# One set's value product turned round, POOL's two steps exchanged, and the quantized product fed earlier

## The chip, the cores and the metric

The kernel runs on one core of one Trainium2 chip. Time is the device time of one execution in microseconds (us); of several runs the median is given. A core has the matrix engine (PE, whose weight loads are shown as PEld), VectorE (DVE), ScalarE (ACT), GpSimd (POOL), and SyncE (SP), which here only issues DMA transfers. PE writes to PSUM[...].

## The reference

A small model of six residual blocks works on x (2 sequences of 64 rows, 1024 columns), with a second input ctx (2 x 1024 x 1024). Each block adds to x a function of its layer norm:

```python
x = x + quantized_matmul(layernorm(x), ctx)          # fake_quant on both operands, per tensor
x = x + mamba(layernorm(x))                          # in_proj, conv, chunk scan, gated norm, out_proj
x = x + lora_experts(layernorm(x))
x = x + point_cloud(ctx, layernorm(x))               # two graph layers
x = x + masked_linear(layernorm(x))
x = x + swiglu_ffn(layernorm(x))
```

Two of them matter here. The quantized product rounds both operands to 256 levels and multiplies: `q = clip(round(x / s + z), 0, 255)`, then `(q1 - z1) * s1 @ (q2 - z2) * s2`.

The point cloud sorts 1024 points of each sequence along four space-filling curves. For each point it takes the 10 neighbours on each curve, and forms features relative to the point itself. In each of two layers a self-attention over the 10 neighbours runs, 64 features a head; its output goes through two linear maps, an instance norm, a leaky ReLU and a maximum over the 10:

```python
scores = einsum('bihd,bjhd->bhij', qh, qh) / sqrt(headdim)
attn = softmax(scores); out = einsum('bhij,bjhd->bihd', attn, qh)
fused = out @ W_lin.T + b_lin;  h1 = einsum('oc,bnkc->bonk', W_conv1, fused)
feats1 = lrelu(instance_norm(h1)).max(axis=-1)
```

Half of the features are the point's own and the same for all its neighbours, so that only four heads need attention; the kernel treats the rest as a constant per point ("centre").

## The kernel before, in words

**Quantized product** (`quant_attention`, L176 to L260). ctx comes in four halves of 2 MB, each as two transfers, into two buffers of the pool `op` (tag "ow"), which later hold output weights; `fetch` (L184) asks for the third and the fourth half when a buffer is free again. ctx is worked on in eight pieces of 128 x 2048. ACT scales a piece (`scaled`, L207), VectorE rounds and clamps it in two instructions to bf16 (`rounded`, L211 and L212), and PE multiplies it twice (L250): with ones, for the column sums (`pc`), and with the quantized, transposed x (`po`). At the end ACT and VectorE add both to x (L254, L255, L258). The small parameters of later blocks are asked for in `parameters` (L262), between the second and the third half of ctx on SP's queue. The weights of `in_proj` follow in `project` (L318) from the pool `wp` (tag "w", three buffers).

**Set-up of the point cloud** (`point_cloud`, L1068). `fused_weights` (L761) multiplies the two linear maps of a layer on the chip and splits the product into three bf16 parts `wz`, whose sum is exact enough. POOL fills the buffers x16 and xz with zeros (L1115).

**The steps.** A phase is one layer of one sequence; there are four, of 22 sets of 48 points each (the last set has 16 points), 88 sets in all. A set's data are 16 blocks of 3 points x 10 neighbours, padded to 32 columns, for two pairs of heads: x of 128 x (2, 16, 32). The set i goes through these functions:

- `edges` (L887, POOL): neighbours minus the centre, into one of four x buffers; `mended` (L895) corrects the first set of a phase.
- `apart` (L908): copies each half of the partitions (one head of each pair) into xz, zeros elsewhere, in one of three buffers. ACT does both halves (L916), but in layer 2 VectorE does the second (L914).
- `scores` (L918, PE), `maxima` (L927, VectorE), `exponentials` (L931: PE subtracts the maxima, L934; ACT takes the exponential, L936).
- `normalize` (L938): VectorE sums and inverts (L941, L942), POOL multiplies e (L943).
- `turn` (L945, VectorE): transposes the attention in 32 x 32 blocks (L947).
- `weighted` (L949): PE forms u = features x wz, per block, with the features as weights and wz as moving operand (L960), three parts one on the other; ACT copies u from PSUM (L962).
- `attend` (L964): PE multiplies attention and u (L975) onto the centres (L972); ACT copies (L977). `back` (L979) transposes it, `collect` (L987) takes norm statistics and maxima on VectorE (L996, L998).

`iteration(i)` (L1146) interleaves them for sets i+2 down to i-3. The order of an engine's instructions comes from this order of calls, with some shifts that the scheduler inside one iteration makes; each engine then runs its list in order. The core of it:

```python
edge(i + 2)                                        # POOL
self.mended(at(i + 1)); self.apart(at(i + 1), 1)
self.turn(at(i - 2)); self.collect(at(i - 3))
self.exponentials(at(i - 1)); self.scores(at(i)); self.normalize(at(i - 1))
self.maxima(at(i)); self.apart(at(i + 1), 0); self.attend(at(i - 2))
self.weighted(at(i)); self.back(at(i - 2)); todo(i)
```

`todo` does what is due beside the steps. The gathers of neighbours for the next phase (L861, POOL's DMA queue, 32 a phase) are turned by PE (L871) and copied by ACT into the window `win` (L868, L873), which `edges` reads. The centres (L829 to L840), the norm of a finished phase (L1021) and the masking of a later weight (L1264) are due there too.

Of the kernel before, what the change touches and what calls it, by code (L numbers as in the profile page):

```python
# [12 lines left out]
BF16 = mybir.dt.bfloat16  # L13
I32 = mybir.dt.int32
AF = mybir.ActivationFunctionType
ALU = mybir.AluOpType
# [4 lines left out]
P = 128  # L21
D = 1024
KC = D // P
NB = 2
S = 64
# [17 lines left out]
NBK = SG // TP  # L43
# [49 lines left out]
class Kernel:  # L93
# [82 lines left out]
    def quant_attention(self, sb, op, gp, rp, ps, pout, ppy):  # L176
# [42 lines left out]
        for b in range(NB):  # L219
            for kp in range(4):  # L220
                j = 2 * b + kp // 2
                if kp % 2 == 0 and j >= 1 and j + 1 < 4:
                    fetch(j + 1)
                v = halves[j][:, 2 * (kp % 2):2 * (kp % 2) + 2, :].rearrange("p k n -> p (k n)")
                scaled(v, 1)
                if b == 0 and kp == 0:
                    scaled(h, 0)
                cq = self.t(gp, [P, 2, D], BF16, tag="xc")
                rounded(cq.rearrange("p k n -> p (k n)"), v)
                if b == 0 and kp == 0:  # L230
                    rounded(hq, h)
                    pt = self.t(ps, [P, KC, P], BF16, tag="misc")
                    for c in range(KC):
                        nc.tensor.transpose(pt[:, c, :], hq[:, c * P:(c + 1) * P], id16)
                    nc.scalar.copy(hT, pt)
                if b == 0 and kp == 1:

                    pr = self.t(ps, [P, 1], tag="misc")
                    for c in range(KC):
                        nc.tensor.matmul(pr, hT[:, c, :], ones16[:, 0:1], start=(c == 0), stop=(c == KC - 1))  # L240
                    dd = self.t(sb, [P, 1], tag="dd")
                    nc.vector.tensor_scalar(dd, d[:, 1:2], float(D), None, ALU.mult)
                    nc.vector.tensor_tensor(row, pr, dd, ALU.add)
                    nc.vector.tensor_tensor(row, row, d[:, 3:4], ALU.mult)
                r = slice(S * b, S * (b + 1))
                for dst in (pc, po):
                    for k2 in range(2):
                        kc = 2 * kp + k2
                        for n in range(2):
                            nc.tensor.matmul(dst[r, n, :], ones16 if dst is pc else hT[:, kc, r], cq[:, k2, 512 * n:512 * (n + 1)],  # L250
                                             start=(kc == 0), stop=(kc == KC - 1))
# [28 lines left out]
    def mamba(self):  # L280
# [3 lines left out]
        with ExitStack() as es:  # L284
# [6 lines left out]
            update = self.quant_attention(sb, op, gp, rp, ps, pout, ppy)  # L291
# [469 lines left out]
    def fused_weights(self, layer):  # L761
# [11 lines left out]
        nc.sync.dma_start(wv, a[f"W_conv{layer}"])  # L773
        wz = [self.t(self.g_w, [P, 2, o], BF16, tag=f"wz{layer}{j}") for j in range(3)]
# [13 lines left out]
        nc.vector.tensor_copy(wctr, pt[:65])  # L788
        return wz, wctr
# [159 lines left out]
    def weighted(self, it):  # L949

        nc, xz, nb, layer = self.nc, it["xz"], it["nb"], it["layer"]
        wz, _ = self.gw[layer]
        u = it["u"] = self.t(self.g_a, [P, NBK, 64 * layer], tag="u", bufs=2)
        kb = 8 // layer
        for k0 in range(0, nb, kb):
            pu = self.t(self.g_ps, [P, kb, 64 * layer], tag="misc")
            for k in range(kb):
                for j in range(3):
                    for hp in range(2):
                        nc.tensor.matmul(pu[64 * hp:64 * hp + 64, k, :], xz[:, hp, k0 + k].rearrange("p a j -> p (a j)"), wz[j][:, hp, :],  # L960
                                         start=(j == 0), stop=(j == 2), skip_group_check=True)
            nc.scalar.copy(u[:, k0:k0 + kb], pu)  # L962

# [104 lines left out]
    def point_cloud(self):  # L1068
        nc, tc, a = self.nc, self.tc, self.a
        with ExitStack() as es:  # L1070
# [69 lines left out]
            def edge(i):  # L1140
                it = at(i)
                if it:
                    it["x"], it["xz"] = x16[i % len(x16)], xz[i % len(xz)]
                    self.edges(it)

            def iteration(i):  # L1146


                edge(i + 2)
# [257 lines left out]
```

## Time and profile before

| | us |
|---|---|
| median of 3 runs (lowest to highest) | 1133.85 (1132.46 to 1140.82) |
| profiled execution, its own time | 1180.42 |
| its span | 1178.6 |
| first matmul of in_proj (L325) | at 49.12 |
| step 0 of layer 1 (L934) | at 551.20 |
| step 0 of layer 2 (L934) | at 800.30 |
| last step of layer 2 (L934) | at 1084.60 |

| stage | us | PE | DVE | ACT | POOL | mean PE clock |
|---|---|---|---|---|---|---|
| quantized product, to 49.12 | 49.12 | 24.11 | 30.59 | 21.97 | 0.20 | 1.00 |
| mamba and experts, to 501.60 | 452.48 | 437.15 | 308.53 | 210.17 | 96.76 | 0.99 |
| set-up of the point cloud | 49.60 | 17.07 | 18.29 | 13.85 | 30.13 | 0.57 |
| layer 1 | 249.10 | 206.67 | 143.49 | 193.17 | 189.08 | 0.92 |
| layer 2 | 284.30 | 266.44 | 208.84 | 205.34 | 180.14 | 0.98 |
| the rest | 94.00 | 85.31 | 28.12 | 11.99 | 1.66 | 0.98 |

A line of a group reads: line, engine, operation, tiles written and read, shapes, how often; then busy us and mean ns of one; then the engine's idle time just before these instructions and what ended it. Line numbers are those of the kernel before. The chain of waits gives start, length, and the work or wait that the end hung on. A releaser is inferred; where several waits end together, the last one is named.

### The profile page before, as it was taken

The page shows a single profiled execution, that of the slowest core. Times are in us where ns is not written, and L with a number is a line of the kernel's source. Part 1 is how long each engine was busy: PE and PEld are TensorE (multiplying, and loading weights), DVE is VectorE, ACT ScalarE, POOL GpSimd, SP SyncE. Part 2 cuts the span into 40 slices and gives each one's busy share as a digit, 9 for nine tenths or more (in the row PEclk, how much of TensorE's full clock was granted, in tenths as well). Part 3 has the DMA queues.
Part 4 walks back from the last instruction along what each step waited for, and adds up shares of the span by engine and source line. Part 5 has one row for each costly group of instructions (what it writes and reads, how often), then busy time and mean ns, then how long its engine had stood idle before and what let it go on. Part 6 is the DMA issues. An engine that isn't in the chain of part 4 may idle for free.

```text
span 1178.6 us, 40925 instructions
## 1 busy us (share of the span) xinstructions
PE 1036.7 (88%) x18413; PEld 796.2 (68%) x18413; DVE 737.9 (63%) x1546; ACT 656.5 (56%) x1057; POOL 498.0 (42%) x403
## 2 busy tenths in 40 slices
PE   3799999999999998944887888888999998999998
PEld 1699968869778683533665666667778776878443
DVE  5698966775766755442554565757757658997511
ACT  4433426556565561025886787865877677776110
POOL 0010110110415245346878877765757657852000
PEclk9999999999999999965998988988999999999999
DMA  6777739677695667475011003110121100000360
GB/s 258 297 286 287 328 145 411 248 299 319 242 402 216 288 240 254 168 221 80 13 23 26 14 12 66 24 27 11 32 44 21 26 11 10 12 4 4 144 285 18
DMA packets 48027, 171.41 MB, mean 145 GB/s; under 512 B 26422, under 2 KB 27362, under 8 KB 40940
## 3 DMA queue, kind: packets, MB, share of 16 engines
q1 hardware_dynamic: 37844, 151.74, 34.8%
q10 hardware_dynamic: 3864, 12.82, 3.0%
q0 software_dynamic: 6144, 4.24, 1.8%
q8 instruction: 144, 2.36, 0.8%
q14 instruction: 31, 0.25, 0.1%
HBM read 163.57 MB, written 2.72 MB: 141 GB/s over the span
## 4 chain that ended last, share of the span: by engine, by line
PE 55%; DVE 22%; ACT 9%; issue 6%; POOL 4%; DMA 4%; SPq 0%; ACTq 0%; another core or an unknown queue 0%; DVEq 0%; POOLq 0%
PE misc L960 13%; PE pin L325 8%; PE po L459 7%; PE op L975 5%; DVE cpre L340 4%; PE sc L925 4%; ACT df L732 3%; PE pt L985 3%; PE sc L1288 2%; DVE df L731 2%; POOL x L893 2%; PE misc L1288 2%; PE sc L934 2%; POOL e L943 2%; PE op L972 1%
## 5 line engine op out<-in xcount | busy, mean ns | idle before, releaser
L325 PEld LDWEIGHTS pin<-hT,w 128*128 128x128 f32 x2320 | 260.9, 192 | 4.5 <-issue 3.8
L325 PE MATMUL pin<-hT,w 128*128 128x128 f32 x2320 | 263.0, 275 | 0.9 <-issue 0.4
L960 PE MATMUL misc<-wz,xz 128*64 128x64 bf16 (+1 forms) x8256 | 213.3, 213 | 17.7 <-issue 14.2
L960 PEld LDWEIGHTS <-xz 128*64 128x64 f16 x8256 | 197.9, 115 | 34.4 <-issue 30.4
L893 POOL TENSOR_TENSOR x<-win,cen 128x960 f16<-128x960 f32 x88 | 170.7, 1946 | 73.0 <-PE sc L925 28.6
L962 ACT COPY u<-misc 128x512 f32<-128x512 f32 x258 | 148.6, 586 | 61.3 <-PE misc L960 34.1
L861 POOL DMA_INDIRECT sl<-src,place x128 | 128.1, 1001 | 40.6 <-issue 18.5
L916 ACT COPY xz<-x 64x1024 f16<-64x1024 f16 (+1 forms) x132 | 134.7, 1020 | 8.1 <-POOL x L893 3.4
L947 DVE STREAM_TRANSPOSE at<-e 128x512 f32<-128x512 f32 x88 | 61.4, 698 | 110.9 <-POOL e L943 110.9
L943 POOL TENSOR_TENSOR e<-e,z 128x512 f32<-128x512 f32 x88 | 95.3, 1083 | 75.2 <-DVE z L942 65.9
L439 POOL TENSOR_TENSOR xc<-y,normw 128x512 f32<-128x512 f32 x8 | 8.3, 1036 | 274.1 <-DVE y L437 231.5
L732 ACT ACTIVATE df<-df,neg 128x1024 f32<-128x1024 f32 x64 | 73.4, 1147 | 90.0 <-DVE df L731 85.5
L459 PE MATMUL po<-ow,xc 128*128 128x512 f32 x256 | 115.3, 604 | 1.7 <-DVE acc L467 1.4
L975 PE MATMUL op<-u,at 128*32 128x64 f32 (+1 forms) x2752 | 92.9, 256 | 22.0 <-issue 13.0
L340 DVE SCALAR_TENSOR_TENSOR cpre<-craw,convw,cpre 128x126 f32<-128x126 f32 (+2 forms) x240 | 78.2, 347 | 28.1 <-ACT cpre L334 20.1
L925 PEld LDWEIGHTS <-xz 128*64 128x64 f16 x2752 | 55.8, 115 | 52.4 <-issue 50.7
L975 PEld LDWEIGHTS op<-u,at 128*32 128x32 f32 x2752 | 64.4, 112 | 39.2 <-issue 21.5
L459 PEld LDWEIGHTS po<-ow,xc 128*128 128x128 f32 x256 | 48.2, 193 | 57.8 <-issue 55.2
L715 POOL DMA_INDIRECT place<-cst,rank x64 | 68.2, 1065 | 40.4 <-issue 17.2
L731 DVE SCALAR_TENSOR_TENSOR df<-hi_r,hl,lo_r 128x1024 f32<-128x1024 f32 x64 | 81.7, 1304 | 4.1 <-DMA lo_r<-rows 2.9
L925 PE MATMUL sc<-x,xz 128*64 128x32 f16 x2752 | 68.0, 186 | 7.8 <-ACT xz L916 5.9
L941 DVE TENSOR_REDUCE z<-e 128x16 f32<-128x512 f32 x88 | 58.8, 668 | 22.3 <-ACT e L936 21.1
(327 smaller groups left out, 1398.2 us busy)
## 6 DMA issues: line engine op xcount, KB each, us to landing
w<-in_in_proj_w SPq DMA_DIRECT2D x36, 2048.0 KB
ow<-in_out_proj_w SPq DMA_DIRECT2D x16, 2048.0 KB
w<-in_L_ffn_w SPq DMA_DIRECT2D x3, 4096.0 KB
ow<-in_ctx SPq DMA_DIRECT2D x8, 1024.0 KB
hi_r<-rows ACTq DMA_DIRECT2D x8, 512.0 KB
lo_r<-rows ACTq DMA_DIRECT2D x8, 512.0 KB
df<-in_L_attn_mask ACTq DMA_DIRECT2D x8, 512.0 KB
w<-in_base_W SPq DMA_DIRECT2D x2, 2048.0 KB
```

Source lines behind the costliest of these rows:

```text
L325: nc.tensor.matmul(pt[:, c, :], w[:, c, kc, :], hT[:, kc, :], start=(kc == 0), stop=(kc == KC - 1))
L340: nc.vector.scalar_tensor_tensor(pv[:, :, s:], rv[:, :, :S - s], convw[:, cc + c, 3 - s:4 - s], pv[:, :, s:], ALU.mult, ALU.add)
L459: nc.tensor.matmul(st["po"][:, n, :], st["xc"][:, 4 * q + c, :], ow[:, c, 512 * n:512 * n + 512], start=(q == 0 and c == 0), stop=(q == 1 ...
L732: nc.scalar.activation(df, df, AF.Sign, bias=neg[:, cc:cc + 1], scale=1.0, accum_out=sums[:, c:c + 1])
L861: nc.gpsimd.indirect_dma_start(out=ph[c][:, m, :], out_offset=None, in_=ph["src"][:, :], in_offset=bass.IndirectOffsetOnAxis(ap=k, axis=0))
L893: nc.gpsimd.tensor_tensor(xv, over, mid, ALU.subtract)
L916: nc.scalar.copy(dst, src)
L925: nc.tensor.matmul(sc[64 * hp:64 * hp + 64, k, :], xz[:, hp, k].rearrange("p a j -> p (a j)"), x[:, hp, k, :], start=False, stop=False, sk ...
L943: nc.gpsimd.tensor_tensor(e, e, z.unsqueeze(2).to_broadcast([P, nb, 32]), ALU.mult)
L960: nc.tensor.matmul(pu[64 * hp:64 * hp + 64, k, :], xz[:, hp, k0 + k].rearrange("p a j -> p (a j)"), wz[j][:, hp, :], start=(j == 0), stop= ...
L962: nc.scalar.copy(u[:, k0:k0 + kb], pu)
L975: nc.tensor.matmul(op[32 * r:32 * r + 32, q, :], it["at"][:, 4 * q + r, :], it["u"][:, 4 * q + r, :], start=False, stop=True, skip_group_c ...
```

## The change

Four things change.

1. The four halves of ctx are all asked for at the start, the third and fourth into two buffers of the weight pool `wp`; so all eight transfers stand ahead of the parameters on SP's queue. ACT scales a piece one ahead. PE's product with x (`po`) is held back one piece, until the transposed x is there. The copy of the transposed x and the three small sums for `row` stand later in ACT's and VectorE's order. `pc` is read and added in two halves.
2. For layer 1 `fused_weights` also lays the weights out by head, 64 rows of values and 64 of zeros, in `heads`: a memset on POOL and six copies on VectorE.
3. For layer 1 `weighted` takes these weights as the stationary operand, 32 columns for each of the four heads, and x itself, 512 columns, as the moving one. Each head's 32 output columns land on 32 partitions of PSUM of their own. `turn_u` then transposes them on VectorE, in 32 x 32 blocks, from PSUM into u; ACT copies nothing. Layer 2 is as before.
4. In both layers `edge(i + 2)` stands after `normalize(at(i - 1))` in `iteration`, no longer first.

```diff
         def fetch(j):
-            c = self.t(op, [P, 4, D], tag="ow")
+            c = self.t(op, [P, 4, D], tag="ow") if j < 2 else self.t(wp, [P, 4, D], tag="w")
...
-        fetch(0)
-        fetch(1)
+        for j in range(4):
+            fetch(j)
         self.parameters(sb, rp)
...
+        scaled(piece(0), 1)
+        scaled(h, 0)
+        for i in range(2 * 4):
+            b, kp = divmod(i, 4)
+            if i + 1 < 8:
+                scaled(piece(i + 1), 1)
+            if i == 1:
+                nc.scalar.copy(hT, pt)
+            cq = self.t(gp, [P, 2, D], BF16, tag="xc")
+            rounded(cq.rearrange("p k n -> p (k n)"), piece(i))
...
+            product(pc, b, kp, cq)
+            waiting.append((po, b, kp, cq))
+            if i >= 1:
+                while waiting:
+                    product(*waiting.pop(0))
...
-        nc.scalar.activation(t, pc.rearrange("p a n -> p (a n)"), AF.Identity, bias=row, scale=d[:, 1:2])
-        nc.vector.scalar_tensor_tensor(self.x, t, s12, self.x, ALU.mult, ALU.add)
+        for q in range(2):
+            c = slice(512 * q, 512 * q + 512)
+            nc.scalar.activation(t[:, c], pc[:, q, :], AF.Identity, bias=row, scale=d[:, 1:2])
+            nc.vector.scalar_tensor_tensor(self.x[:, c], t[:, c], s12, self.x[:, c], ALU.mult, ALU.add)
...
+        if layer == 1:
+            heads = self.t(self.g_w, [P, 3, 2, 2, o], BF16, tag="wzh")
+            nc.gpsimd.memset(heads, 0.0)
...
+        if layer == 1:
+            for j in range(3):
+                for h2 in range(2):
+                    r = slice(64 * h2, 64 * h2 + 64)
+                    nc.vector.tensor_copy(heads[r, j, :, h2, :], wz[j][r])
+            wz = heads
...
+        if layer == 1:
+            u = self.t(self.g_a, [P, 2, NBK, 32], tag="u", bufs=2)
+            it["u"] = u.rearrange("p a b o -> p b a o")
+            for ob in range(2):
+                pu = self.t(self.g_ps, [P, NBK, 32], tag="misc")[:, 0:nb]
+                for j in range(3):
+                    for h in range(4):
+                        nc.tensor.matmul(pu[32 * h:32 * h + 32], wz[:, j, h // 2, h % 2, 32 * ob:32 * ob + 32], it["x"][:, h // 2, 0:nb, :],
+                                         start=(j == 0), stop=(j == 2), skip_group_check=True)
+                it["pu"].append((u[:, ob, 0:nb], pu))
+            return
...
+    def turn_u(self, it):
+        for u, pu in it["pu"]:
+            self.nc.vector.transpose(u.rearrange("p b j -> p (b j)"), pu.rearrange("p b j -> p (b j)"))
...
-                edge(i + 2)
                 if at(i + 1):
                     self.mended(at(i + 1))
                     self.apart(at(i + 1), 1)
...
                 if at(i - 1):
                     self.normalize(at(i - 1))
+                edge(i + 2)
                 if at(i):
                     self.maxima(at(i))
...
                 if at(i):
                     self.weighted(at(i))
+                    self.turn_u(at(i))
```

More of the change, by code (lines that the diff above doesn't have):

```diff
@@ L173, in transposed, with quant_attention @@
         return hT
-    def quant_attention(self, sb, op, gp, rp, ps, pout, ppy):
+    def quant_attention(self, sb, wp, op, gp, rp, ps, pout, ppy):
         nc, a = self.nc, self.a
@@ L218, in quant_attention @@
         pc = self.t(ppy, [P, 2, 512], tag="py")
[L219 to L251, printed above, removed]
@@ new lines, in quant_attention, with product @@
+        waiting = []
+        def product(dst, b, kp, cq):
+            r = slice(S * b, S * (b + 1))
+            for k2 in range(2):
+                kc = 2 * kp + k2
+                for n in range(2):
+                    nc.tensor.matmul(dst[r, n, :], ones16 if dst is pc else hT[:, kc, r], cq[:, k2, 512 * n:512 * (n + 1)],
+                                     start=(kc == 0), stop=(kc == KC - 1))
+        piece = lambda i: halves[i // 2][:, 2 * (i % 2):2 * (i % 2) + 2, :].rearrange("p k n -> p (k n)")
@@ new lines, in quant_attention @@
+        scaled(piece(0), 1)
[8 more added lines that the diff above has]
+            rounded(cq.rearrange("p k n -> p (k n)"), piece(i))
+            if i == 0:
+                rounded(hq, h)
+                pt = self.t(ps, [P, KC, P], BF16, tag="misc")
+                for c in range(KC):
+                    nc.tensor.transpose(pt[:, c, :], hq[:, c * P:(c + 1) * P], id16)
+            product(pc, b, kp, cq)
[3 more added lines that the diff above has]
+                    product(*waiting.pop(0))
+            if i == 1:
+                pr = self.t(ps, [P, 1], tag="misc")
+                for c in range(KC):
+                    nc.tensor.matmul(pr, hT[:, c, :], ones16[:, 0:1], start=(c == 0), stop=(c == KC - 1))
+            if i == 2:
+                dd = self.t(sb, [P, 1], tag="dd")
+                nc.vector.tensor_scalar(dd, d[:, 1:2], float(D), None, ALU.mult)
+                nc.vector.tensor_tensor(row, pr, dd, ALU.add)
+                nc.vector.tensor_tensor(row, row, d[:, 3:4], ALU.mult)
@@ L290, in mamba @@
             es.enter_context(tc.manual_schedule(engines=WITH_SP))
-            update = self.quant_attention(sb, op, gp, rp, ps, pout, ppy)
+            update = self.quant_attention(sb, wp, op, gp, rp, ps, pout, ppy)
             convw, convb, normw = self.convw, self.convb, self.normw
@@ L1142, in edge @@
                 if it:
+                    it["pu"] = []
                     it["x"], it["xz"] = x16[i % len(x16)], xz[i % len(xz)]
```

## The prediction

> **What bounds the kernel now.** I read the table of stages first, cut at the matmul that subtracts the maxima (L934), which runs once in each of the 88 steps of the point cloud: steps 0 to 43 (layer 1) from 551.2 us, steps 44 to 87 (layer 2) from 800.3 to 1084.6 us.
>
> ```profile
> core 0: us, PE busy (x) PEld busy (x) DVE busy (x) ACT busy (x) POOL busy (x), PEclk, DMA share, GB/s
> 551.20:800.30 249.10, 206.67 (x7130) 161.83 (x7128) 143.49 (x295) 193.17 (x310) 189.08 (x151) 0.92 0.12 25
> 800.30:1084.60 284.30, 266.44 (x7260) 220.40 (x7260) 208.84 (x341) 205.34 (x347) 180.14 (x136) 0.98 0.09 18
> ```
>
> A step takes 249.1/43 = 5.79 us in layer 1 and 284.3/43 = 6.61 us in layer 2. In layer 2 PE is busy 94% of the time. In layer 1 no engine is full (PE 83%, ACT 78%, POOL 76%), so a chain between engines sets the step, and PE loses time to itself. The groups of layer 1, with the idle time ahead of them in the last column, say which:
>
> ```profile
> L947 DVE STREAM_TRANSPOSE at<-e 128x512 f32<-128x512 f32 x41 | 29.1, 711 | 63.8 <-POOL e L943 63.7
> L893 POOL TENSOR_TENSOR x<-win,cen 128x960 f16<-128x960 f32 x42 | 82.3, 1968 | 27.8 <-ACT win L873 13.7 <-PE sc L925 9.0 <-remote 2.7
> L975 PE MATMUL op<-u,at 128*32 128x64 f32 x1328 | 39.1, 230 | 18.0 <-issue 11.1 <-DVE at L947 6.4
> ```
>
> VectorE's transpose of the attention waits 63.7 us for POOL's normalized e, because POOL does the edges of a later set ahead of it. PE waits 11 us here, and 11 us in the product of u, for "issue". On the chain of waits "issue" is 13.1% of layer 1 and 4.5% of layer 2: 33 + 13 = 45 us.
>
> The quantized product is bound at first by one landing of data, then by a second one that was asked for late; the chain:
>
> ```profile
> 1.65 7.72 DMA ow<-in_ctx
> ...
> 27.89 6.95 DMA ow<-in_ctx
> 34.87 2.10 ACT ow L207
> 36.99 1.24 DVE ow L211
> 38.33 1.24 DVE xc L212
> ```
>
> **What the Trainium skill says.** "TensorE: Matmul & The Clock Gate", Architectural detail: ScalarE's and VectorE's queues are strict FIFO, only PE pulls weight loads ahead. The timeline agrees: both engines run in the program's order, waiting ones included. My main step rests on it. The same page, Part 3: outputs of 32 columns in different column strips run at the same time, three strips 2.38 times as fast as one. The trace agrees: 32 matmuls of L975 in four strips take 0.58 us on the chain, 18 ns each. "SBUF — State Buffer", Who interferes with whom: a VectorE operation with at most one SBUF input outside the two-port modes does not fight POOL for ports. The transpose out of PSUM is such a one; that it reads PSUM no row of before shows, but L947 is 0.70 us with POOL beside it. The first page, Part 1: PE's clock halves after an idle window of about 3.4 us; the trace shows the granted clock at 0.5 in several windows of layer 1 (mean 0.92).
>
> **Part 1, the quantized product.** All eight loads of ctx (1 MB each) are issued at once, two buffers coming from the weight pool. Piece 0 still lands at 9.4 us; at the 415 GB/s of the busy slices a piece takes 2.5 us, so the last lands at 27 instead of 34.9. VectorE needs 1.23 + 1.23 us a piece: from 15.4 us (piece 0 and h done) seven pieces are 17.2 us, with three small ones 33.0, against 39.6 before: -6.6. The y in halves lets VectorE's first half run under ACT's second: -0.5. So **-7** (bounds -8, as in landing at once, and -5, if loads side by side are slower). On SP's queue the seven parameter loads and the first weights now stand behind the ctx loads; parameters are used from 58 us (L334) and land before 27. Of the three weight loads that lie ready at 49 us, the second and third now wait for VectorE's last reading of buffers 2 and 3 (27.7 and 33 us); 2 MB takes 5 us, so they land at about 34 and 39, ahead of PE's first use at 42. If that cover went, PE would wait a few us.
>
> **Part 2, set-up.** Six copies of 0.2 us (as L788) on VectorE, which is the chain there: **+1** (0 to 1.5). POOL's memset of 768 columns, 0.8 us (L1115: 1.0 for 1024), lies before 13.6 us of POOL idle: nothing.
>
> **Part 3, u of layer 1.** PE: 96 matmuls of 64 columns, 1.64 us, become 24 of 512. A 512-column bf16 matmul follows its neighbour in 0.22 us (L934 to L922), so in four strips 6 x 0.22 = 1.3 us: -0.3, between 1.3 and, strip after strip, 5.3. 144 fewer PE instructions of 336 a step should take about half of the "issue" waits of layer 1, some 12 us, off PE. ACT: two copies of 0.587 go, -1.17. VectorE: two transposes of 0.71 (bounds 0.655, the reduction L929 from PSUM, and 1.0) come, after waiting for PE; behind them is queued the turn of the next attention, on which L975 waits. VectorE's sum is then 0.71 + 0.39 + 0.39 + 0.68 + 0.25 + 0.66 + 1.42 = 4.5 us, below the step. All of this would gain if the step were PE's or ACT's. It is not:
>
> **Part 4, POOL's order.** Edges(i+2) now stand behind the normalization of i-1. That e comes early, as wanted, but it closes a circle. Edges(i+2) cannot start before e(i-1). In the next step ACT's first instruction is the copy of those edges (L916), and in its queue the exponential of i stands behind it; VectorE's z(i) and POOL's e(i) follow, and then edges(i+3). One turn is one step. Before, edges stood first and a turn spanned two steps. Steps from start to start:
>
> ```profile
> 553.22 0.60 ACT L936 ACTIVATE e<-sc 128x512 f32<-128x512 f32 x1
> 553.84 1.05 ACT L916 COPY xz<-x 64x1024 f16<-64x1024 f16 x1
> 553.85 0.69 DVE L941 TENSOR_REDUCE z<-e 128x16 f32<-128x512 f32 x1 [7.37 <-ACT e L936]
> 554.57 0.25 DVE L942 RECIPROCAL z<-z 128x16 f32<-128x16 f32 x1
> 554.79 0.57 ACT L962 COPY u<-misc 128x512 f32<-128x512 f32 x1
> 554.97 1.05 POOL L943 TENSOR_TENSOR e<-e,z 128x512 f32<-128x512 f32 x1 [3.38 <-ACT xz L916]
> ...
> 1004.00 0.70 DVE L947 STREAM_TRANSPOSE at<-e 128x512 f32<-128x512 f32 x1
> 1004.74 0.42 DVE L914 COPY xz<-x 64x1024 f16<-64x1024 f16 x1
> 1005.17 0.67 DVE L996 BATCH_NORM_STATS2 st<-pt 128x6 f32<-128x480 f32 x1
> 1005.76 0.64 DVE L998 TENSOR_REDUCE hm<-pt 128x48 f32<-128x480 f32 x1
> 1006.43 0.69 DVE L941 TENSOR_REDUCE z<-e 128x16 f32<-128x512 f32 x1
> 1007.15 0.25 DVE L942 RECIPROCAL z<-z 128x16 f32<-128x16 f32 x1
> ```
>
> Layer 1: edges 1.97 + 0.03 to the waiter, copy 0.95, exponential 0.63, sum 0.72, reciprocal and hop 0.40, e until the edges start 1.01 (744.48 to 745.49): **5.71 us**. Every 2.7 steps ACT's win copy (L873, 0.39) stands in it: 0.14. VectorE has 1.2 us to spare, but its tasks between sets take up to 2.6 us: I take 0.1 (0 to 0.3). So 5.95 x 43 = 256 us, **+7**. Gathers (1.48 a step of 1.28) fit into POOL's wait of 2.7 us. Layer 2: the copy goes by VectorE, ahead of all else: 2.00 + 0.43 + 0.74 + 0.59 + 0.67 + 0.72 + 0.40 + 1.01 = **6.56 us**. With 0.15 for overruns 6.7 x 40, and three steps without edges at 5.77 (the last ones of before), 285 us: **+1**.
>
> **Sum.** -7 + 1 + 7 + 1 = +2 against the profiled execution's 1180.4 us. But the median of the runs is 1133.85, 46.6 us less. The two circles hold no PE instruction, only ACT, VectorE and POOL at work, so they stay as long in a run that PE gets through faster. What PE loses by "issue" on the chain of these two stages is 45 us, of the size of the gap. If all the gap lies there, the loops of before take 533 - 45 and the change costs 47 us; if it is spread evenly, 2. I take half: 1133.85 + 2 + 22 = **1158 us**.
>
> **Rivals.**
> *The circles bind, but no more than the present step (1136).* The gap of 46.6 us lies elsewhere. For it: layer 1's 5.79 is nearly 5.95 already. Against: steps of 5.4 in a row near 645 us and 5.77 at the end show what the engines do undisturbed.
> *A gain: POOL's early e frees the chain (1098).* If the wait of L947 for e is what ends last, layer 1 falls to POOL's own sum, 1.20 + 1.97 + 1.48 x 1.28 = 5.07: 43 x 0.72 = -31, with -7 + 1 that is -37 on 1180, or 1098 on the median. It speaks for it that the wait is the largest of the stage. It decides only where ACT's copy does not wait for the edges, so that 0.65 us of the circle are hidden; the in-order queue excludes that as I read it.
> *Strips do not overlap (about 1230).* Then u costs 5.3 us, PE's step is 7.7 against 5.95, 43 x 1.75 = +75. Against it: L975's 18 ns.
>
> **Numbers.** Forecast 0.59, no more than the present step 0.28, gain 0.09, strips 0.04. Between runs of this kernel about 1% (1122.5 to 1145.2) cannot be told from no change. Slower 0.62, same 0.27, faster 0.11. The range goes from the rival's 1136 less the bounds of parts 1 and 4 (-1 and -8) to the whole gap in the loops with PE at half clock a little more often (1181 + 3): 1127 to 1184.
>
> **What would show it.** Right: first use of in_proj weights (L325 before) at about 42 us; the interval of the maxima matmul near 5.9 in layer 1 with little spread, near 6.6 or more in layer 2; ACT's copy and, in layer 2, VectorE's copy waiting for POOL's edges for tens of us; POOL's e waiting for z; PE's busy share in both stages lower. Wrong: a layer 1 step below 5.6, which would mean the circle is not closed; a product of u over 3 us on PE; or weights late at 42 us.

## The result: slower by 49 us

| | us |
|---|---|
| kernel before, in the same set of runs | 1137.34 (1132.46 to 1141.15) |
| changed kernel | 1186.31 (1184.75 to 1186.62) |
| ratio | 1.043, 95% interval 1.038 to 1.048 |
| profiled execution of the changed kernel, its own time | 1186.53 (span 1184.8) |

The forecast was 1158 with a range of 1127 to 1184: the sign was right, the size half of what came. Runs sent together share a chip, and each ratio below is taken against the kernel before among them; that kernel takes 1134 to 1139 us (medians) in some of these sets and 1176 to 1179 in others, which turns out to be the heart of the matter. I call them short sets and long sets; this result is of a short one.

### The profile page after: what moved, and what is told of

It is laid out like the page before. It is cut to its first block, busy times and chain, and to the rows that moved or that the text cites. A ratio compares the mean times of both kernels' runs of the same rounds, so it can differ in the third digit from the quotient of the medians.

```text
span 1184.8 us, 34694 instructions
## 1 busy us (share of the span) xinstructions
PE 1013.4 (86%) x15341; PEld 743.2 (63%) x15341; DVE 757.0 (64%) x1641; ACT 612.6 (52%) x972; POOL 503.4 (42%) x404
## 4 chain that ended last, share of the span: by engine, by line
PE 29%; DVE 27%; POOL 19%; ACT 13%; issue 5%; DMA 5%; ACTq 0%; POOLq 0%; SPq 0%; DVEq 0%
POOL x L912 13%; PE pin L335 8%; POOL e L962 6%; PE po L469 5%; ACT xz L935 4%; DVE cpre L350 4%; ACT df L742 3%; PE sc L1325 2%; PE misc L991 2%; DVE z L960 2%; DVE at L966 2%; DMA df<-in_L_attn_mask 2%; DVE df L741 2%; PE misc L1325 2%; ACT e L955 2%
## 5 line engine op out<-in xcount | busy, mean ns | idle before, releaser
L912 POOL TENSOR_TENSOR x<-win,cen 128x960 f16<-128x960 f32 x88 | 180.4, 2050 | 2.9 <-ACT win L892 2.8
L962 POOL TENSOR_TENSOR e<-e,z 128x512 f32<-128x512 f32 x88 | 90.5, 1028 | 151.5 <-DVE z L961 102.0
L880 POOL DMA_INDIRECT sl<-src,place x128 | 130.7, 1021 | 42.4 <-issue 17.4
L991 PE MATMUL misc<-wz,xz 128*64 128x128 bf16 x4128 | 125.9, 221 | 1.9 <-ACT u L993 1.0
L991 PEld LDWEIGHTS <-xz 128*64 128x64 f16 x4128 | 118.6, 111 | 11.0 <-issue 10.8
L1010 PE MATMUL op<-u,at 128*32 128x64 f32 (+1 forms) x2752 | 83.1, 268 | 46.6 <-DVE at L966 46.4
L993 ACT COPY u<-misc 128x512 f32<-128x512 f32 x172 | 100.4, 586 | 19.8 <-PE misc L991 11.5
L350 DVE SCALAR_TENSOR_TENSOR cpre<-craw,convw,cpre 128x126 f32<-128x126 f32 (+2 forms) x240 | 78.1, 347 | 28.1 <-ACT cpre L344 22.4
L1020 PE MATMUL pt<-cst,oT 128*128 128x128 f32 x258 | 49.0, 298 | 43.6 <-ACT oT L1012 43.6
L944 PEld LDWEIGHTS <-xz 128*64 128x64 f16 x2752 | 55.4, 117 | 46.8 <-issue 46.8
L980 PE MATMUL misc<-x,wzh 128*32 128x512 f16 (+1 forms) x1056 | 81.9, 455 | 0.6 <-ACT win L892 0.6
```

Of the source, the lines that this page charges most:

```text
L350: nc.vector.scalar_tensor_tensor(pv[:, :, s:], rv[:, :, :S - s], convw[:, cc + c, 3 - s:4 - s], pv[:, :, s:], ALU.mult, ALU.add)
L880: nc.gpsimd.indirect_dma_start(out=ph[c][:, m, :], out_offset=None, in_=ph["src"][:, :], in_offset=bass.IndirectOffsetOnAxis(ap=k, axis=0))
L912: nc.gpsimd.tensor_tensor(xv, over, mid, ALU.subtract)
L962: nc.gpsimd.tensor_tensor(e, e, z.unsqueeze(2).to_broadcast([P, nb, 32]), ALU.mult)
L1010: nc.tensor.matmul(op[32 * r:32 * r + 32, q, :], it["at"][:, 4 * q + r, :], it["u"][:, 4 * q + r, :], start=False, stop=True, skip_group_c ...
```

## The profile after

The stages, cut at the first in_proj product and at the matmul that subtracts the maxima (L953 now). Columns: start and end, length, busy time and instructions of each engine, PE's granted clock, DMA share, GB/s. By count the cut between the two layers lies at the last step of layer 1 (step 43), and the second ends one step before the last; so it was in the table of before too (800.30 and 1084.60), and all kernels here are cut alike.

```profile
core 0: us, PE busy (x) PEld busy (x) DVE busy (x) ACT busy (x) POOL busy (x), PEclk, DMA share, GB/s
...
543.50:806.70 263.20, 194.29 (x4132) 115.95 (x4129) 185.36 (x381) 145.75 (x225) 186.68 (x149) 0.86 0.11 22
806.70:1091.90 285.20, 259.48 (x7260) 217.51 (x7259) 183.47 (x343) 208.75 (x347) 192.35 (x139) 0.99 0.09 18
```

Layer 1 is 263.2 us, 6.12 a step, and layer 2 285.2. PE is busy 74% and 91% of the two; no engine is full in layer 1. The groups of layer 1 (busy time, mean ns of one | idle time just before and what ended it) say where the waiting went:

```profile
L935 ACT COPY xz<-x 64x1024 f16<-64x1024 f16 x80 | 83.4, 1042 | 102.3 <-POOL x L912 94.7 <-DVE x L922 6.8
L912 POOL TENSOR_TENSOR x<-win,cen 128x960 f16<-128x960 f32 x40 | 78.5, 1963 | 0.0
...
L962 POOL TENSOR_TENSOR e<-e,z 128x512 f32<-128x512 f32 x42 | 44.0, 1048 | 64.0 <-ACT xz L935 36.5 <-DVE z L961 23.3 <-ACT oT L1012 4.2
...
L966 DVE STREAM_TRANSPOSE at<-e 128x512 f32<-128x512 f32 x41 | 27.9, 680 | 1.8 <-POOL e L962 1.7
```

In the kernel before, ACT's copy and POOL's e of layer 1 waited far less:

```profile
L916 ACT COPY xz<-x 64x1024 f16<-64x1024 f16 x80 | 83.3, 1042 | 4.7 <-POOL x L893 3.4
L943 POOL TENSOR_TENSOR e<-e,z 128x512 f32<-128x512 f32 x42 | 45.5, 1082 | 18.0 <-DVE z L942 14.3 <-ACT xz L916 3.4 <-issue 0.2
```

VectorE's wait of 63.7 us for e is gone, as POOL's order was to bring about; in its place ACT's copy waits 94.7 us for POOL's edges and POOL's e 64 us, for ACT and VectorE mostly. One turn of the circle, on the chain of waits of layer 1 (start, length, work):

```profile
633.08 1.05 POOL e L962
634.12 1.93 POOL x L912
636.05 0.02 issue
636.08 1.04 ACT xz L935
637.12 0.03 issue
637.14 0.60 ACT e L955
637.74 0.02 issue
637.77 1.05 ACT xz L935
638.82 0.01 POOLq L962
638.83 0.10 issue
638.92 1.05 POOL e L962
```

A turn is 638.92 - 633.08 = 5.84 us without a PE instruction in it. The chain puts ACT's second copy last before e; VectorE's sum and reciprocal (0.68 + 0.25) end within 0.1 us of it. In layer 2 the same is seen on VectorE; the first line is of the kernel before:

```profile
L975 PE MATMUL op<-u,at 128*32 128x128 f32 x1296 | 48.8, 280 | 3.5 <-DVE at L947 1.8 <-issue 1.4
...
L1010 PE MATMUL op<-u,at 128*32 128x128 f32 x1296 | 45.2, 281 | 22.4 <-DVE at L966 22.4
L962 POOL TENSOR_TENSOR e<-e,z 128x512 f32<-128x512 f32 x42 | 44.0, 1048 | 82.8 <-DVE z L961 74.5 <-ACT oT L1012 6.3 <-ACT xz L935 2.0
...
L933 DVE COPY xz<-x 64x1024 f16<-64x1024 f16 x41 | 17.4, 424 | 90.7 <-POOL x L912 90.7
```

PE, which was the bound of layer 2, now waits 22.4 us for the turned attention, where it waited 1.8.

## The experiments

The theories of the first four runs: **A**, the circle that POOL's late order closes sets the time. **B**, the new u of layer 1 costs it (VectorE's transposes, or PE at half clock). The rivals of later runs stand in their expectations. For the size of the loss a second question came up: what the 46.6 us between the profiled execution and the runs of before are.

### Which part costs

`e1_order_only`: the kernel before with only POOL's order changed.

```diff
-                edge(i + 2)
...
                     self.normalize(at(i - 1))
+                edge(i + 2)
```

> The kernel before with POOL's edges put behind the normalization, nothing else changed. Theory A (the circle edges, ACT's or VectorE's copy, exponential, sum, normalization, edges sets the step): layer 1 steps near 6.1 us, layer 2 steps near 6.6 us in the profile, and the whole 50 to 60 us slower than before, 1187 to 1197 us, since the product's 7 to 8 us are not gained. Theory B (the loss comes from u: VectorE's transposes, or PE at half clock because it has less to do): within 10 us of before, 1127 to 1147 us.

`e3_u_only`: the parts 2 and 3 of the change alone. Against the changed kernel, edges come first again and `quant_attention` is that of before:

```diff
+                edge(i + 2)
                 if at(i + 1):
...
                     self.normalize(at(i - 1))
-                edge(i + 2)
...
-        update = self.quant_attention(sb, wp, op, gp, rp, ps, pout, ppy)
+        update = self.quant_attention(sb, op, gp, rp, ps, pout, ppy)
```

> The kernel before with the new u of layer 1 (and its set-up) alone, POOL's order as before. Theory A: the circle is not there; layer 1 steps fall towards POOL's own 5.1 us in the profile, and the whole is between 25 us faster and the same, 1112 to 1138 us. Theory B: most of the loss is here, 1170 to 1195 us.

`e4_order_undone`: the changed kernel with `edge(i + 2)` first again (the first diff backwards).

> The changed kernel with POOL's edges put first again. Theory A: no loss is left; u_only less 7 us, 1105 to 1131 us. Theory B: still slower than before, 1163 to 1187 us.

`e2_quant_only`: the kernel before with the changed `quant_attention` alone.

```diff
-            c = self.t(op, [P, 4, D], tag="ow")
+            c = self.t(op, [P, 4, D], tag="ow") if j < 2 else self.t(wp, [P, 4, D], tag="w")
```

> The kernel before with the reordered quantized product alone. Both theories: first in_proj matmul at about 43.8 us instead of 49.1, 5 to 8 us faster than before, 1129 to 1132 us. If the early start is given back later in the mamba block, 1137.

| before in this set 1139.22 | us | ratio (95%) | layer 1 | layer 2 |
|---|---|---|---|---|
| e1, order alone | 1228.45 | 1.079 (1.073 to 1.084) | 298.7 | 289.5 |
| e3, u alone | 1145.60 | 1.005 (1.002 to 1.008) | 237.5 | 265.1 |
| e4, all but the order | 1140.92 | 1.002 (1.000 to 1.005) | 233.9 | 265.2 |
| e2, quantized product alone | 1130.96 | 0.992 (0.990 to 0.994) | 233.0 | 264.0 |

The order is the cause: taking it back gives 45 us (1186.31 to 1140.92, both in short sets), adding it alone costs 89. That is far more than theory A's 1187 to 1197, and the trace of e1 says why the changed kernel gets off with less (chain of waits, layer 1):

```profile
699.15 1.92 POOL x L893
701.08 0.02 issue
701.10 1.05 ACT xz L916
702.15 0.02 issue
702.17 1.07 ACT u L962 x2
703.24 0.02 issue
703.26 0.41 ACT pm L868
703.68 0.04 issue
703.72 0.69 PE misc L871 x2
```

In the old form of u ACT's two copies from PSUM stand in its queue behind the copy of the late edges; so the chain runs on from there into PE, and steps of 9 to 12 us come between steps of about 4 to 7. The new u takes those copies off ACT and is worth 298.7 - 263.2 = 36 us of layer 1 under the late order. Under the old order it is worth nothing: layer 1 takes 233.9 us with it (e4) and 233.0 without (e2), and by the medians it costs 6 us (e3 against before) to 10 (e4 against e2), of which the traces place some 3 (1 in the set-up, 1 in each layer). Theory A had counted on a gain there, and so e3 and e4 lie 8 and 10 us above its ranges. Theory B falls: they lie 22 us and more below its own. Why layer 1 does not get shorter there stays open; VectorE is at work for 192 of the 234 us, by 49 us more than without.

The loops (the two layers' steps) of the kernel before, unchanged in e2, are 233.0 and 264.0 us here, not the 249.1 and 284.3 of the profile shown ahead of the prediction:

```profile
540.90:773.90 233.00, 196.50 (x7131) 157.16 (x7129) 143.56 (x295) 192.42 (x310) 190.78 (x151) 0.92 0.14 27
773.90:1037.90 264.00, 257.43 (x7260) 216.67 (x7260) 205.97 (x341) 206.95 (x347) 180.18 (x136) 0.99 0.10 19
```

### What the gap of 46.6 us is

`f1_before_again` is the kernel before, unchanged, with a profile of its own. `g1_after_again` is the changed kernel in another set; neither has an edit.

> The kernel before, unchanged, for a second profile. It decides on the term of +22 in the prediction's sum. Theory A (the first profiled execution was slow in the two loops, and its loops are else as those of the run with the quantized product alone): layer 1 at 5.4 us a step (233 us, not 249), layer 2 at 6.1 (268 us, not 288), profiled time 1133 to 1146. Rival (the profile itself slows PE in this kernel): the profiled time is again 1175 to 1185, with layer 1 near 249 us.

> The changed kernel once more, beside the kernel before on whichever chip this is. The kernel before took 1139 on one chip and 1176 on another. Theory A (the two circles hold no PE instruction, so a chip on which PE is slower to get its work does not lengthen them): 1180 to 1195 on either chip, that is a ratio of about 1.04 where before takes 1139 and about 1.01 where it takes 1176. Rival (the loss of the change is a factor on PE's own time): a ratio of 1.03 to 1.05 on either chip, 1215 to 1235 where before takes 1176.

f1 came in a long set: its profiled execution took 1172.16, with the loops at 239.8 and 281.7 us. That is near the rival's number, but not for its reason, for the timed runs of before in that set took 1176.15 as well; and in the set above the profiled execution of e2 took 1133.93 against a median of 1130.96. So the profile does not lengthen a run. By their times the profiled execution of before and its three runs were of two kinds of set. The best pair for what the kinds differ in is one kernel in both: e2, profiled at 1133.93, and `i2_quant_only_again` (below), profiled in a long set at 1174.47, with these loops:

```profile
547.80:796.10 248.30, 202.29 (x7136) 159.07 (x7128) 143.30 (x295) 192.97 (x311) 192.14 (x152) 0.95 0.13 25
796.10:1079.90 283.80, 265.73 (x7260) 219.55 (x7260) 208.91 (x341) 205.67 (x347) 180.46 (x136) 0.98 0.09 18
```

They are within 1 us of those of the first profile (the one ahead of the prediction), and 35 us (15 and 20) longer than in e2, out of 41 for the whole.

g1 took 1196.75 in a long set, where before took 1175.97: ratio 1.017 (1.008 to 1.025). Across the kinds of set before moves by 37 to 39 us and the changed kernel by 10. Its layer 1 does not move at all; its layer 2 is 6.5 us longer:

```profile
549.30:812.10 262.80, 196.81 (x4132) 117.80 (x4129) 184.66 (x381) 146.27 (x225) 187.26 (x150) 0.86 0.12 22
812.10:1103.80 291.70, 266.73 (x7260) 219.64 (x7259) 184.72 (x343) 207.03 (x347) 192.41 (x138) 0.99 0.09 17
```

1196.75 is 2 us above theory A's range and 18 below the rival's. Part of what the long sets cost the old order shows in layer 1 on PE's product of u and attention; first f1, then e2, groups of layer 1:

```profile
L975 PE MATMUL op<-u,at 128*32 128x64 f32 x1328 | 39.9, 226 | 20.2 <-issue 11.4 <-DVE at L947 8.3
```

```profile
L985 PE MATMUL op<-u,at 128*32 128x64 f32 x1328 | 29.8, 231 | 12.5 <-DVE at L957 11.1 <-issue 1.4
```

The same 1328 matmuls hold PE for 10 us more and wait 10 us more for "issue", at the same duration of one. But "issue" on the chain of waits of both loops is 42 us in i2 and still 36 in e2 (45 in the first profile), so that it accounts for 6 to 10 of the 35 us. In layer 2, 19 of the 20 us lie in steps in which POOL issues gathers; the last eight intervals between steps, which have none, agree to 0.01 us. Why steps with gathers are longer in some sets was not tried and stays open. By the numbers of the chips it is not fixed by the chip: number 15 gave the short set of e1 to e4 and the long one of g1 to g4, and number 7 the short set of h1 to h4 and the long one of i1 and i2.

### Opening the circle

`f2_opened`, `g4_opened_again` and `h4_opened_third` are one kernel in three sets: POOL's order stays late, but the copies move behind the next maxima, so that the exponential no longer stands behind them.

```diff
                     self.mended(at(i + 1))
-                    self.apart(at(i + 1), 1)
...
                 if at(i + 1):
+                    self.apart(at(i + 1), 1)
                     self.apart(at(i + 1), 0)
```

> The changed kernel with both copies of apart moved behind the maxima, POOL's late order kept. The exponential of a set no longer stands behind the copy of edges made in the same turn, so the circle spans two steps. Theory A (the circle sets the time): 1125 to 1150, near the run with the old order (1141), that is 37 to 60 us less than the changed kernel's 1186. Theory B (late edges cost by POOL's own waiting, whatever the copies do): 1175 to 1190.

> The changed kernel with both copies of apart behind the maxima, again, to have it beside the changed kernel on one chip, and on another chip if this is one. Where before takes 1176 it took 1151. Theory A: 1145 to 1155 there again; 1110 to 1132 where before takes 1139, since with the circle open PE is what bounds layer 2 again and gains from the better chip. Rival (opening the circle leaves another bound that holds no PE): 1148 to 1155 on either chip.

`h3_order_undone_again` (the kernel of e4) runs beside the third.

> The changed kernel with the edges first again, beside the opened kernel on one chip. Where before took 1139 it took 1141. If this chip is such a one: 1136 to 1146. Where before takes 1176: the new u takes 3000 PE instructions away, and with them the waits for issue of layer 1, so 1155 to 1172 by Theory A (PE's getting its work is what differs between the chips); the rival (VectorE's two transposes bound layer 1 in the old order) says 1176 to 1185.

> The changed kernel with both copies of apart behind the maxima, once more, for the pair with the kernel whose edges are first. Theory A: 5 to 15 us less than that one on the same chip, from layer 1; the rival (the late place of the edges is never worth anything): no less.

| | before in the set | us | ratio (95%) |
|---|---|---|---|
| f2, opened | 1176.15 | 1151.12 | 0.977 (0.972 to 0.982) |
| g4, opened | 1175.97 | 1154.41 | 0.980 (0.972 to 0.988) |
| h4, opened | 1135.84 | 1129.37 | 0.995 (0.993 to 0.997) |
| h3, edges first | 1135.84 | 1139.12 | 1.003 (1.000 to 1.005) |

In one set (g) the changed kernel takes 1196.75 and the opened one 1154.41: moving the copies is worth 42 us, with POOL's edges just as late. That is the sharpest evidence for the circle, since lateness by itself would have stayed. Against the old order with the same u (h3) it gains 10 us. Against the quantized product alone it gains nothing in a short set (ratios 0.995 for h4 and 0.992 for e2), but some 17 to 21 us in long ones (0.977 and 0.980 against 0.995 for i2 below). The stages of h4:

```profile
542.40:761.30 218.90, 171.08 (x4132) 104.70 (x4129) 187.26 (x379) 145.64 (x225) 186.38 (x149) 0.96 0.14 26
761.30:1032.60 271.30, 256.53 (x7260) 216.11 (x7260) 231.34 (x345) 207.45 (x347) 189.38 (x139) 0.99 0.09 19
```

Layer 1 is 5.09 us a step, 15 us shorter than in h3 (234.0). That is where the rival of a gain had put it (POOL's own sum, 5.07), and why it failed before: its condition was that the copy be out of the way. That POOL's sum is now what bounds the layer isn't shown: POOL is busy for 186 of the 219 us. Layer 2 is 6 us longer than with the old order (265.1). The trace of h4 puts these 6 us into six intervals, steps 72 to 78, which take 41.7 us against 35.6 in h3; each holds a product of the later weight with its mask on VectorE (L1301):

```profile
960.66 1.05 POOL L962 TENSOR_TENSOR e<-e,z 128x512 f32<-128x512 f32 x1 [1.92 <-DVE z L961]
961.06 0.93 DVE L933 COPY xz<-x 64x1024 f16<-64x1024 f16 x1
961.67 2.15 POOL L912 TENSOR_TENSOR x<-win,cen 128x960 f16<-128x960 f32 x1
962.02 2.87 DVE L1301 TENSOR_TENSOR w_attn<-w_attn,on 128x1024 f32<-128x1024 f32 x1
```

There VectorE is busy for 6.9 of the 7.0 us of an interval and bounds it. Beside POOL the mask product takes 2.87 us and the copy 0.93, where in the changed kernel they take 1.84 and 0.42; together 1.5 us more in each interval. No run leaves the masks out of this kernel, so this is read from the trace alone.

`f4_quant_opened`: the same with the old u (e2 with late edges and both copies moved).

> The kernel before with the reordered quantized product, POOL's late order and both copies of apart behind the maxima; u of layer 1 as before. Theory A (with the circle open the place of the edges is worth nothing, or a little of VectorE's 63.7 us of waiting for e): 1110 to 1135, no slower than the quantized product alone (1131). Theory B (the loss of the late order is POOL's waiting, and is larger without the new u): 1190 to 1225.

1163.81 in the set of f2, ratio 0.988 (0.983 to 0.992); it was expected without allowance for the long set, so only the ratio counts, and that is in A's direction. Layer 1 is 244.5 us there against 226.0 with the new u: in the opened circle the new u is worth 18 us.

`i1_opened_layer1`: late edges and moved copies for the sets of layer 1 only (the second argument is the layer), layer 2 as before. `i2_quant_only_again` is the kernel of e2.

```diff
+                edge(i + 2, 2)
...
-                edge(i + 2)
+                edge(i + 2, 1)
```

> The changed kernel with the late order for layer 1 alone, there with both copies behind the maxima; layer 2 in the order of before. Put together from the traces: where before takes 1136, layer 1 of the opened kernel (219, against 234 with the old order) and layer 2 of the old order (269, against 275): 1139 - 15 = 1124, or 1129 - 6 = 1123, so 1118 to 1129. Where before takes 1176, layer 2 is the same in both orders (286), so 1148 to 1156, as the opened kernel. Rival (what layer 1 gains by the late order is given back at the start of layer 2, where its sets meet the old order): no less than the opened kernel's 1129, or 1160 and over where before takes 1176.

> The kernel before with the reordered quantized product alone, once more, so that the two best kernels stand beside each other. It took 0.9921 of before where that takes 1139. Expected: 7 to 10 us less than before on either chip (1126 to 1131, or 1164 to 1170), since the stage ahead of the loops holds no wait for PE's instructions. Rival (the gain of the first run was of the spread between runs): within 3 us of before.

A long set again (before 1178.66): i1 1162.92, ratio 0.985 (0.978 to 0.993), i2 1174.47, ratio 0.995 (0.991 to 0.999). i1 came out as its rival said, and is no better than the opened kernel's 0.977 and 0.980. i2 gained 4 us, between its two expectations.

### The two layers, and what lies in the circle

`f3_late_layer1` and `h1_late_layer2`: the kernel before with late edges for the sets of one layer.

```diff
-                if it:
+                if it and it["layer"] == layer:
```

> The kernel before with POOL's late order for sets of layer 1 alone. With the late order in both layers the trace showed layer 1 at 298.7 us and layer 2 at 289.5 us, against 233 and 264 in the run with the quantized product alone. Theory A (each layer has a circle of its own; in layer 1 ACT's two copies of u stand in it): 1139 + 66 = 1205 (1195 to 1215). Theory B (the loss of layer 1 is carried in from layer 2's late edges, or depends on both): below 1180.

> The kernel before with POOL's late order for sets of layer 2 alone. Theory A (a circle of its own in layer 2, which the mask's products and PE's part do not add to): where before takes 1139, layer 2 goes from 264-268 to 285-290, so 1156 to 1166; where before takes 1176, layer 2 is at 286 already and goes to 287-292, so 1174 to 1184. Rival (layer 2's loss was carried in from layer 1): no change from before on either chip.

f3: 1230.75 against 1176.15, layer 1 at 301.9 us: as long as in e1's short set (298.7), so it hardly depends on the kind of set. The expected 1205 was added to a short set's 1139; the 66 us became 55 in the main because the old order's layer 1 is itself longer here (239.8 in f1). h1: 1158.80 against 1135.84, +23, with layer 1 at 229.5 and layer 2 at 286.9, inside theory A's 1156 to 1166. Each layer has its own circle.

`g2_half_edges` and `h2_half_edges_before`: POOL's edges for one head pair only, in the changed kernel and in the one before. `g3_no_mask`: the changed kernel without the weight's mask products.

```diff
-        nc.gpsimd.tensor_tensor(xv, over, mid, ALU.subtract)
+        nc.gpsimd.tensor_tensor(xv[:, 0:1], over[:, 0:1], mid[:, 0:1], ALU.subtract)
```

> The changed kernel with POOL's edges made for one of the two head pairs only (the other pair's are left out, so x holds less than the reference's), 0.9 us less a set; all else is as in the changed kernel. Theory A (edges lie in the circle of both layers): 0.7 to 0.9 us a step until the next bound (PE's 5.77 in layer 2): 40 to 65 us less, 1121 to 1146 where the changed kernel takes 1186. Rival (POOL is not in what sets the step): within 10 us of the changed kernel.

> The kernel before with POOL's edges made for one of the two head pairs only (the other pair's are left out), the same cut that took 45 us off the changed kernel. Theory A (in the old order the edges are a set ahead and lie in no circle of one step; only what POOL's early e saves is gained): 0 to 15 us less than before. Rival (shorter edges help in either order alike): 40 us less or more.

> The changed kernel without the eight products of the attention weight with its mask on VectorE (left out, so the masked weight is not formed), which fall in eight of the last steps of layer 2, where the edges take 2.94 us instead of 1.97. Theory A (they stretch the edges by 0.97 us, and these lie in the circle): 7 to 10 us less than the changed kernel. Rival (VectorE has the time to spare, the stretched edges are hidden): within 3 us.

g2: 1152.14 against 1196.75, 45 us less, 31 of them in layer 1 (231.6 against 262.8). h2: 1112.25 against 1135.84, 24 us less, above theory A's 15 and below the rival's 40. So the edges weigh more in the late order (31 us of layer 1 against 21, 233.0 in e2 to 212.1 in h2), but they are not free in the old one: VectorE's wait for e, which the edges delay, falls with them from 64 us in e2 to 45 in h2, and so is likely part of what set layer 1. g3: 1188.67 against 1196.75, 8 us less, as expected; that is eight times the 0.98 us by which the edges are stretched in the timeline of the changed kernel:

```profile
1008.96 1.84 DVE L1301 TENSOR_TENSOR w_attn<-w_attn,on 128x1024 f32<-128x1024 f32 x1
1009.68 2.94 POOL L912 TENSOR_TENSOR x<-win,cen 128x960 f16<-128x960 f32 x1
```

VectorE's mask product starts first and ends at 1010.80; the edges, 1.96 us elsewhere, take 2.94. In the late order POOL's edges always start just after VectorE is free to begin such a product, so all eight are hit, and the turn is 7.29 us instead of 6.31. The Trainium skill, "SBUF — State Buffer", Who interferes with whom, says that a VectorE operation with two SBUF inputs contends with a GpSimd operation that reads SBUF, and that the ports they share are an exclusive lock. The trace agrees: the 0.98 us are nearly what was left of the product (1.12); and in h4, where the edges start first, it is the product that is stretched, by 1.03 us.

## Why the prediction was right in sign and short in size

**Part 1 (-7): right in size, with a slip.** The first in_proj product came at 43.78, not 42. The chain:

```profile
14.58 0.71 DVE hq L212
15.33 1.04 PE misc L244 x8
16.37 3.39 PE py L226 x8
19.76 0.88 PE po L226 x4
20.66 1.23 DVE xc L212
```

VectorE waits for PE at the second piece, which the sum left out; from there a piece takes 2.47 us as worked out. e2 gained 8.3 us, and i2, in a long set, 4.2, a little less than the lower bound of 5.

**Part 2 (+1): right.** Step 0 of layer 1 starts at 541.9 us in e4 and 540.9 in e2.

**Part 3: right in its sizes.** VectorE's transpose out of PSUM took 691 ns (0.71 taken). The 24 matmuls hold PE 1.48 us at full clock and 2.79 at a granted clock of 0.50 (1.3 taken); first a line of h4, then one of the changed kernel:

```profile
600.21 1.48 PE L980 MATMUL misc<-x,wzh 128*32 128x512 f16 x24
...
690.19 2.79 PE L980 MATMUL misc<-x,wzh 128*32 128x512 f16 x24
```

The strips do overlap, and that rival falls. ACT's busy time fell by 47 us, and the "issue" ahead of the attention product in layer 1 is nearly gone, in a long set too (1.7 us in g1 against 11.4 in f1). What the prediction did not see is how these copies stand to the circle: the late order costs 89 us with the old u and 45 with the new.

**Part 4 (+7 and +1): right in mechanism.** Layer 2 was forecast at 285 and is 285.2 (291.7 in the long set of g1). Layer 1 was forecast at 256 and is 263.2: a turn alone is 5.84, not 5.71, and overruns come to 0.28 a step instead of 0.24. In layer 2 the size is right by chance: an undisturbed turn is 6.31, not 6.56, some steps are still PE's 5.77, and the mask products' 8 us, which were not named, fill the rest.

**The gap: the step that failed.** Against the profiled execution the sum was +2, and the profiles differ by +6; but that compares a profile of the long kind with one of the short kind. Within the long kind, g1's stages add up to some 20 us more than the first profile's: the start comes 2 us earlier instead of 6, layer 1 is 14 longer instead of 7, layer 2 7 instead of 1. The prediction went on: "If all the gap lies there, the loops of before take 533 - 45 and the change costs 47 us; if it is spread evenly, 2. I take half". So it put the loops of before at 511 us in the runs and those of the changed kernel at 541, +30. The loops of before take 497 us in a short set, 36 less than in the profile, and those of the changed kernel 548: +51. Of the 21 us that are missing, 14 are the mis-sized term, +22 where the loops show +36, and 7 are the turn of layer 1. With the loops starting 5 us earlier (548.6 in e1, 543.5 now), +51 makes +46, near the 49 measured; the last 3 are not placed.

So most of the gap (36 of 46.6 us) lay in the loops of before, as the prediction's first case had it, and the loops of the changed kernel came out no shorter than the circles that were worked out from the long profile. That this case's 47 us come so near the 49 is in part luck: its 45 is 9 too many, and layer 1's 7 are missing. The argument for it was half right. That the circles hold no PE instruction held: layer 1 takes 263.2 us in one kind of set and 262.8 in the other. That what PE lost to "issue" had the gap's size (45 us) was a coincidence, for 36 us of it are still on the chain in a short set. Halving was a guess between two bounds, with no measurement behind it. The range stopped 2 us short for the same reasons: its upper end took the gap in full, but not the 7 us of layer 1 beside it.

**The rivals.** "The circles bind, but no more than the present step" (a ratio of 1.002) was wrong in both kinds of set: it is 1.043 in the short ones and 1.017 (1.008 to 1.025) in the long ones. "A gain" was wrong for this kernel; for layer 1 of the opened one its step of 5.07 us was right, and the whole gained 6 to 25 us where it forecast 36. (Its own sum, 1133.85 - 37, gives 1097, not 1098.)

## What to carry to other kernels

When the profiled execution and the timed runs of one kernel differ by more than its runs do among themselves, find out in which stage the difference lies, and price a change against that stage as it is in the runs. A new chain that sets the step need not shrink with it: here layer 1 of the changed kernel took the same in both kinds of set. Before an engine's instruction is moved later to serve one reader, follow its other reader to the next instruction behind it in that reader's in-order queue, and on until the path comes back: if it comes back within one step, its lengths add up to a floor for the step. Here the early e was worth having only once the copy was moved as well, and in a short set not even then more than the quantized product alone.

## What was not expected of the hardware

- The kernel before takes 1134 to 1139 us in some sets and 1176 to 1179 in others, each within 1.5% or so; one kernel's loops took 497 us in the one kind and 532 in the other, 19 of the 20 us of layer 2 in steps with gathers, and two chips showed both kinds. A kernel whose steps are set by ACT, VectorE and POOL moved by 10 us only.
- Four column strips side by side: 24 matmuls of 512 columns and 32 outputs start and end within 1.48 us, where the page "TensorE: Matmul & The Clock Gate" of the Trainium skill, Part 3, has three strips at 2.38 times one. One after the other at the 0.22 us of a full-width neighbour they would take 5.3 by estimate, so this is 3.6 times.
- VectorE's copy of 64 x 1024 in f16 takes 424 ns where it follows the edges (changed kernel) and 928 (median) in h4, where it runs beside POOL's e and the start of the edges; the edges of layer 2 grow there from 1.96 to 2.15 us (median), and a VectorE product of 128 x 1024 beside them from 1.84 to 2.87.
